# A layer norm's square root taken from the activation table, and the second block's norm moved ahead of the feed-forward steps, in an attention and feed-forward kernel

## The chip, the core and the metric

The kernel runs on one core of a Trainium2 chip. The metric is the device time of one execution in microseconds (us). The engines are named as the profile names them: PE (TensorE's matmuls) and PEld (its weight loads), DVE (VectorE), ACT (ScalarE), POOL (GpSimd), and SP (SyncE), whose queue issues nearly all of the transfers. Each engine works through its own instructions strictly in the order in which the program gives them; an instruction that waits for another engine holds up everything behind it on its own engine.

## The reference

The input x has 8 sequences of 256 tokens with 512 features, 2048 tokens in all. What is computed, shortened:

```python
xn = _layernorm(x, axis=-1)                  # (x - m) / sqrt(v + 1e-5)
s = attn(xn)                                 # latent attention, 128 heads, head size 4, rope part 64
g = _silu(ffn(xn))                           # gate = silu(lin1(xn)); up = lin3(xn); lin2(gate * up)
return x + s * g

def lin(x, wq, A, B):                        # each of lin1, lin2, lin3
    w = jnp.tile(wq, (1, 4))
    return x @ w.T + (x @ A.T @ B.T) * 0.5
```

Because the weight is tiled four times, a product with it is a product of the sum of the four quarters of x with `wq`. The kernel uses this: it sums the quarters first.

## The kernel before

**First phase and attention.** The kernel has two parts. `first_phase` handles the norm, the low-rank parts and the whole feed-forward network (FFN); it writes the gates g and the projected latents to DRAM. The attention over 64 pairs of (sequence, group of heads) follows and takes most of the time. The change touches the first phase alone, which covers about the first 200 us of the span, and within it what happens up to about 45 us.

**Blocks and tiles.** `first_phase` works on four blocks `tb` = 0 to 3 of 512 tokens. A block of x is four tiles `xt_tb_n` of 128 tokens by 512 features (`load_x`). The tag `xt` has six buffers, so four tiles of block 0 and two of block 1 have room at once; the third and the fourth tile of block 1 wait until tiles of block 0 have been transposed.

**The norm.** `norm_part(tb, n)` takes mean and variance of one tile on DVE (L416, L417). `norm(tb)` does this for four tiles and then finds 1/sqrt(variance + eps) for 128 x 4 values at once. It starts from the guess by a shifted integer (L428, L430) and improves it by three Newton steps: for block 0 as nine small DVE instructions (L436 to L438), for the other blocks as twelve small POOL instructions (L440 to L443), with two more (L449, L450) for the offset `off` = -mean/deviation. `norm_one(tb, n)` then normalizes a tile in place, on DVE for block 0 (L459), on ACT for the others (L457, which reads `off`). `turn(tb)` transposes the four tiles on PE, and ACT and DVE copy the results out of PSUM (L470, L472).

**Sums and narrow products.** `sums(tb)` adds the four quarters of the features: `xs0` on DVE (L479), `xs2` on POOL (L480), and their sum on DVE (L481). `narrow(tb)` makes the low-rank parts (`pm` on PE, `mid` on DVE L497), sends two rows through DRAM to spread them over all partitions (`low`), and `down(tb)` makes the latents (`pp`) and, on POOL, four differences for the attention (L158).

**Removing the first row.** Before block 0's FFN the weights `w1_sb` and `w3_sb` are changed once: the first row of `wq` is spread over the partitions by small PE products (`spread_first`, L627), copied by ACT into `first_0` and `first_1` (L635, L651), and subtracted by `less_first` (L641, L643: POOL for `w1_sb`, DVE for `w3_sb`) and `rest_less_first` (L652, L655, POOL). `first_0` and `first_1` lie in the two buffers of the tag `hT`, which the FFN needs afterwards.

**The FFN.** `main(tb, u)` is one of six steps of a block, each with two chunks of 128 hidden units (the last with one). Per chunk PE makes `px` and `py` in two PSUM banks, DVE adds the low-rank part to each (L541 for `gate`, L545), ACT applies SiLU to `gate` (L544), and the product of the two is made by POOL (L558) or DVE (L556). In steps 0 and 1 of block 0 both products are DVE's, and `py` is kept in PSUM until then. The tag `gate` has two buffers, PSUM has eight banks. `fold` (POOL) and `low_out` (PE, L582) follow after steps 3 and 5; `gate_out` makes the block's output (`pf`).

**The order.** Nothing is scheduled automatically (`tc.manual_schedule()`): the order of the Python calls is the order on each engine. Around the change the calls run thus: 26 transposes of a constant on PE (`warm(26)`); four `spread_first` with their copies; `warm(2)`; `norm(0)`; four `norm_one(0, n)`; `turn(0)`; `sums(0)`; `less_first(0)` on POOL; `narrow(0)`; `less_first(1)` on DVE; `down(0)`; `rest_less_first`; and then the loop over blocks and steps. In this loop, block 1's norm stands behind step 1 of block 0:

```python
if u == 1 and tb == 0:
    stats = norm(1)
if more:
    for n in range(4):
        if u == (n if tb else 2 + n // 2):
            norm_one(tb + 1, n, *stats)
```

SP's queue issues, in this order: block 0's four tiles, small weights, `wdn_sb`, ten loads of `w1_sb` and `w3_sb`, six small loads of `chunk_rows`, block 1's four tiles, and then `narrow(0)`'s transfers.

Of the kernel before, what the change touches and what calls it, by code (L numbers as in the profile page):

```python
# [9 lines left out]
F32 = mybir.dt.float32  # L10
I32 = mybir.dt.int32
AF = mybir.ActivationFunctionType
ALU = mybir.AluOpType
# [3 lines left out]
P = 128  # L17
# [20 lines left out]
def mla_ffn_gate_kernel(  # L38
# [19 lines left out]
    nc = tc.nc  # L58
# [255 lines left out]
    def first_phase(between):  # L314
# [13 lines left out]
        f2 = pool("f2", 2, st)  # L328
        xts, xns, xnT, xsum, lows = {}, {}, {}, {}, {}

        def load_x(tb):
            xts[tb] = []
            for n in range(4):
                t = f1.tile([P, D], F32, tag="xt", name=f"xt_{tb}_{n}", bufs=6)
                nc.sync.dma_start(out=t, in_=x[ds(tb * TB + n * P, P), :])
                xts[tb].append(t)

        def by_chunks(to, of):

# [18 lines left out]
        nc.scalar.dma_start(out=rows[64:97:32], in_=b13[0:33:32, :])  # L358
        for k, wt in enumerate((w1t, w3t)):
            nc.scalar.dma_start(out=rows[65 + 32 * k : 66 + 32 * k], in_=wt[0:1, :])  # L360
        chunk_rows = f2.tile([P, TB], F32, tag="gs", name="chunk_rows")[:, 0:P]
        nc.gpsimd.memset(chunk_rows[0:32], 0.0)

# [26 lines left out]
        nc.sync.dma_start(out=wdn_sb, in_=w_down.rearrange("(c p) m -> p c m", p=P))  # L390
        for w_sb, wt in ((w1_sb, w1t), (w3_sb, w3t)):
            load_chunks(nc.sync, w_sb, wt)

        of = b13[1:34:32, :].rearrange("k (q f) -> q k f", q=4)
        for n in range(2):
# [5 lines left out]
        for m in range(3):  # L401
# [2 lines left out]
                out=chunk_rows[16 + 2 * m : 18 + 2 * m, 96 : 96 + w],  # L404
                in_=of[3, :, ds(256 + 32 * m, w)],
            )
        load_x(1)

        mvs = {}

        def norm_part(tb, n):

            if n == 0:
                mvs[tb] = f2.tile([P, 4, 2], F32, tag="mv", name=f"mv_{tb}")
            s6 = f2.tile([P, 6], F32, tag="st", name=f"st_{tb}_{n}")
            nc.vector.bn_stats(s6, xts[tb][n])  # L416
            nc.vector.bn_aggr(mvs[tb][:, n, :], s6)  # L417

        def norm(tb):


            for n in range(4):
                norm_part(tb, n)
            mv = mvs[tb]
            ve = f2.tile([P, 4], F32, tag="ve", name=f"ve_{tb}")
            nc.vector.tensor_scalar_add(ve, mv[:, :, 1], EPS)
            i0 = f2.tile([P, 4], I32, tag="i0", name=f"i0_{tb}")
            nc.vector.tensor_single_scalar(i0, ve.bitcast(I32), 1, ALU.logical_shift_right)  # L428
            r0 = f2.tile([P, 4], I32, tag="r0", name=f"r0_{tb}")
            nc.vector.tensor_scalar(r0, i0, -1.0, float(0x5F3759DF), ALU.mult, ALU.add)  # L430
            r = r0.bitcast(F32)
            e = f2.tile([P, 4], F32, tag="e", name=f"e_{tb}")
            for step in range(3):
                new = f2.tile([P, 4], F32, tag=f"r{step}", name=f"r_{tb}_{step}")
                if tb == 0:
                    nc.vector.scalar_tensor_tensor(e, r, -0.5, r, ALU.mult, ALU.mult)  # L436
                    nc.vector.scalar_tensor_tensor(e, e, 1.0, ve, ALU.mult, ALU.mult)
                    nc.vector.scalar_tensor_tensor(new, e, 1.5, r, ALU.add, ALU.mult)  # L438
                else:
                    nc.gpsimd.tensor_mul(e, r, r)  # L440
                    nc.gpsimd.tensor_mul(e, e, ve)
                    nc.gpsimd.tensor_scalar(e, e, -0.5, 1.5, ALU.mult, ALU.add)
                    nc.gpsimd.tensor_mul(new, e, r)  # L443
                r = new

            off = None
            if tb:
                off = f2.tile([P, 4], F32, tag="off", name=f"off_{tb}")
                nc.gpsimd.tensor_mul(off, mv[:, :, 0], r)  # L449
                nc.gpsimd.tensor_scalar(off, off, -1.0, None, ALU.mult)  # L450
            return mv, r, off
# [22 lines left out]
        def sums(tb):  # L474

            a = xnT[tb]
            xs = [f1.tile([P, TB], F32, tag=f"xs{k}", name=f"xs{k}_{tb}") for k in range(2)]
            xs2 = f1.tile([P, TB], F32, tag="tmp", name=f"xs2_{tb}")
            nc.vector.tensor_add(xs[0], a[:, 0, :], a[:, 1, :])  # L479
            nc.gpsimd.tensor_add(xs2, a[:, 2, :], a[:, 3, :])  # L480
            nc.vector.tensor_add(xs[0], xs[0], xs2)  # L481
            nc.scalar.copy(xs[1], xs[0])
            xsum[tb] = xs
# [142 lines left out]
        def spread_first(k, ps, one, two):  # L626
            nc.tensor.matmul(  # L627
                ps, others[64 + 32 * k : 66 + 32 * k], two, start=True, stop=True, skip_group_check=True
            )
            return one, ps  # L630

        for i in range(2):
            for k in range(2):
                ps = bank(f"first_{k}_{i}").rearrange("p (q m) -> p q m", q=2)
                nc.scalar.copy(*spread_first(k, ps, *parts[k][i]))  # L635
        warm(2)

        def less_first(k, engine):
            w_sb = (w1_sb, w3_sb)[k]
# [14 lines left out]
                one = w_sb[:, 8:11][:, a, b]  # L654
                nc.gpsimd.tensor_sub(one, one, firsts[k][:, 8:11][:, a, b])  # L655

        stats = norm(0)
        for n in range(4):
            norm_one(0, n, *stats)
        turn(0)  # L660
        sums(0)
        less_first(0, nc.gpsimd)
        narrow(0)
        less_first(1, nc.vector)
        between(-1)
        for to, of in ((a2_sb, a2), (w2_sb, w2t), (w2_sb[96:98, 2, :], b2[0:2, :])):
            nc.sync.dma_start(out=to, in_=of)
# [3 lines left out]
        nc.scalar.copy(bcol_sb.rearrange("p c k -> p (c k)"), ps)  # L671
        rest_less_first(0)
        rest_less_first(1)
        for tb in range(NTB):
            more = tb + 1 < NTB
            for u in range(6):
                pj = None
                if not more and u >= 2:
                    pj = Project(u - 2)
                    pj.start()  # L680
                main(tb, u)
                if pj:
                    pj.second()
                    pj.end()
                if u in (3, 5):
                    fold(tb, u // 2 - 1)
                    low_out(tb, u // 2 - 1)
                if u == 1 and tb == 0:
                    stats = norm(1)
                if more:  # L690
                    for n in range(4):
                        if u == (n if tb else 2 + n // 2):
                            norm_one(tb + 1, n, *stats)
                if u == 4 and more:
# [429 lines left out]
```

## Time and profile before

| What | us |
|---|---|
| Median of 3 runs | 1986.38 (1986.12 to 1987.19) |
| The profiled execution's own time | 1985.42 |
| Span of that execution, first to last instruction | 1983.6 |
| PE busy in the span | 1966.4 |
| From 11 to 37 us: PE busy | 25.89 of 26.00 |
| From 37 to 50 us: PE busy | 8.60 of 13.00 |
| From 50 to 66 us: PE busy | 16.00 of 16.00 |
| From 200 to 1970 us: PE busy | 1768.37 of 1770.00 |

The rows for stretches come from the windows of the profile. They say where TensorE has gaps at all: at the very start, between 37 and 50 us, a little in each later block of the first phase, and hardly ever in the attention. ACT loads an activation table three times (L635 at 4.02 us, L544 at 23.77 us, and L717 ahead of the attention), 1.28 us each. PE's granted clock is full in all but a few microseconds of the span (mean 0.999).

### The profile page before, as it was taken

The numbers are of one execution on the slowest core, as the hardware profiler recorded it, in microseconds if no ns is written. First come the engines' busy times: TensorE is split into PE (matmuls) and PEld (weight loads), VectorE is DVE, ScalarE is ACT, GpSimd is POOL, SyncE is SP. The second block draws the span as 40 slices with busy tenths as digits, with TensorE's granted clock in tenths as the row PEclk, the third lists the DMA queues.
The fourth block names the chain that finished last, engine by engine and source line by source line (L and its number), as shares of the span: only waits on it lengthen the run. The fifth ranks groups of instructions, "written<-read, shape, count | busy, mean of one in ns | idle before, by whom it ended". The sixth has DMA issues, their size and how long they took to land.

```text
span 1983.6 us, 86719 instructions
## 1 busy us (share of the span) xinstructions
PE 1966.4 (99%) x38065; PEld 1402.2 (71%) x38065; DVE 1570.7 (79%) x2666; ACT 1091.5 (55%) x2987; POOL 759.1 (38%) x1113
## 2 busy tenths in 40 slices
PE   8999999999999999999999999999999999999998
PEld 4334577777777767777777767777777767777775
DVE  6764678888787877788787877788787878888888
ACT  3333556556556555556556555556556555655654
POOL 5876545554552323232332323232332323232232
PEclk9999999999999999999999999999999999999999
DMA  6235322212232223221232223221232222222212
GB/s 195 100 118 181 112 88 87 88 67 87 88 126 77 100 87 109 93 87 66 87 113 80 100 87 107 94 88 66 88 110 82 99 88 87 67 88 87 74 49 87
DMA packets 120048, 187.53 MB, mean 95 GB/s; under 512 B 10715, under 2 KB 84843, under 8 KB 119673
## 3 DMA queue, kind: packets, MB, share of 16 engines
q1 hardware_dynamic: 119665, 181.97, 26.7%
q8 instruction: 301, 4.93, 1.0%
q14 instruction: 74, 0.61, 0.1%
q10 hardware_dynamic: 8, 0.02, 0.0%
HBM read 147.86 MB, written 34.10 MB: 92 GB/s over the span
## 4 chain that ended last, share of the span: by engine, by line
PE 92%; POOL 3%; DVE 2%; issue 1%; DMA 1%; ACT 0%; SPq 0%; POOLq 0%; ACTq 0%; DVEq 0%
PE q L173 40%; PE sc L824 35%; PE av L870 11%; PE po L173 2%; PE pf L173 1%; PE py L173 1%; PE px L173 1%; PE qq L249 1%; POOL h4b L571 0%; DVE pt L853 0%; POOL h L570 0%; POOL hT L558 0%; DMA xt<-in_x_dram 0%; DMA gate_d<-gs 0%; POOL h L572 0%
## 5 line engine op out<-in xcount | busy, mean ns | idle before, releaser
L843 ACT ACTIVATE pr<-sc,nmx 128x256 f32<-128x256 f32 x2048 | 814.4, 500 | 470.3 <-DVE nmx L837 466.0
L837 DVE TENSOR_REDUCE nmx<-sc 128x2 f32<-128x512 f32 x1024 | 635.7, 683 | 289.1 <-PE sc L824 265.0
L853 DVE STREAM_TRANSPOSE pt<-pr 128x512 f32<-128x512 f32 x1024 | 635.1, 678 | 0.0
L216 POOL TENSOR_TENSOR e<-e,e 128x256 f32<-128x256 f32 x128 | 93.9, 733 | 1045.2 <-ACT e L211 559.3
L824 PE MATMUL sc<-act,qr 32*128 32x256 f32 x8192 | 489.0, 374 | 0.0
L173 PE MATMUL q<-x,ws 128*32 128x256 f32 x8192 | 488.9, 379 | 0.0
L824 PEld LDWEIGHTS sc<-act,qr 32*128 32x128 f32 x8192 | 421.2, 185 | 21.9
L173 PEld LDWEIGHTS q<-x,ws 128*32 128x32 f32 x8192 | 266.3, 110 | 175.7
L173 PE MATMUL q<-x,w 128*32 128x256 f32 x6144 | 381.6, 381 | 0.7 <-DVE py L545 0.7
L173 PEld LDWEIGHTS q<-x,w 128*32 128x32 f32 x6144 | 187.1, 110 | 155.7 <-ACT pr L843 35.9
L824 PE MATMUL sc<-kc,qcm 32*128 32x256 f32 x4096 | 281.3, 387 | 0.2 <-issue 0.2
L870 PE MATMUL av<-pt,vpad 128*32 128x128 f32 x8192 | 235.9, 273 | 0.1
L870 PEld LDWEIGHTS av<-pt,vpad 128*32 128x32 f32 x8192 | 226.3, 110 | 12.6 <-issue 1.6
L824 PEld LDWEIGHTS sc<-kc,qcm 32*128 32x128 f32 x4096 | 198.2, 184 | 52.2 <-issue 39.4
L211 ACT COPY e<-q 128x256 f32<-128x256 f32 x512 | 202.2, 396 | 25.9 <-PE q L173 25.8
L890 ACT ACTIVATE acc<-av,sides_sb 128x256 f32<-128x256 f32 (+1 forms) x130 | 54.2, 469 | 247.0 <-PE av L870 247.0
L269 POOL TENSOR_TENSOR qcm<-qc,mask_sb 128x1024 f32<-128x1024 f32 x64 | 122.2, 1910 | 0.0
L218 POOL TENSOR_TENSOR qr<-e,e 128x256 f32<-128x256 f32 x128 | 93.6, 731 | 10.0
L217 POOL TENSOR_TENSOR e<-e,e 128x256 f32<-128x256 f32 x128 | 93.6, 731 | 10.0
L310 POOL COPY vpad<-vall 32x128 f32<-32x128 f32 x256 | 74.9, 293 | 10.7 <-PE av L870 2.7
L228 DVE TENSOR_TENSOR qr<-e,q 128x256 f32<-128x256 f32 x128 | 53.9, 421 | 22.4 <-POOL e L216 17.0
L541 DVE SCALAR_TENSOR_TENSOR gate<-low,bcol_sb,px 128x512 f32<-128x512 f32 x44 | 32.8, 745 | 45.0 <-POOL hT L558 24.7
(124 smaller groups left out, 1133.7 us busy)
## 6 DMA issues: line engine op xcount, KB each, us to landing
w<-in_w_rope_dram SPq DMA_DIRECT2D x128, 512.0 KB
ws<-sums_d SPq DMA_DIRECT2D x96, 512.0 KB
sums_d<-ws SPq DMA_DIRECT2D x32, 512.0 KB
x<-xs_d SPq DMA_DIRECT2D x28, 256.0 KB
xt<-in_x_dram SPq DMA_DIRECT2D x16, 256.0 KB
xs_d<-xt SPq DMA_DIRECT2D x16, 256.0 KB
gate_d<-gs SPq DMA_DIRECT2D x16, 256.0 KB
g<-gate_d SPq DMA_DIRECT2D x16, 256.0 KB
```

Source lines behind the costliest of these rows:

```text
L173: nc.tensor.matmul(to[tile_], w[:, tile_], x, start=start, stop=stop, skip_group_check=True)
L211: nc.scalar.copy(self.e[i], self.banks[i])
L216: nc.gpsimd.tensor_add(m6, m6, m1)
L217: nc.gpsimd.tensor_add(m7, m7, m6)
L218: nc.gpsimd.tensor_add(self.out(1, 1), self.split(m7), self.split(m5))
L269: nc.gpsimd.tensor_mul(qcm, qks[b, sg // 2][0].rearrange("p (q i) -> p q i", i=32).unsqueeze(2).to_broadcast([P, 8, 4, 32]), mask_sb[:, ds ...
L310: nc.gpsimd.tensor_copy(vpad[rows, :, :, 8 * t + 4 * (sg % 2) :][..., :4], valls[b][rows, :, sg])
L824: nc.tensor.matmul(sc[r][:, h, :], lhs.rearrange("p t i -> p (t i)"), rhs, start=(part == 0 and h == 0), stop=(part == 2), skip_group_chec ...
L837: nc.vector.tensor_reduce(nmx[:, r, :], scs[n, f][r], AX.X, ALU.max, negate=True)
L843: nc.scalar.activation(p[:, h, :], scs[n, f][r][:, h, :], AF.Exp, bias=nmxs[n, f][:, r, h : h + 1])
L853: nc.vector.transpose(pts[n, f // 2, r].rearrange("p k q i -> p q k i")[:, ds(2 * (f % 2), 2)], prs.pop((n, f, r)).rearrange("p h (k j) -> ...
L870: nc.tensor.matmul(av[32 * r : 32 * r + 32, ds(half * P, P)], vpad[:, k, r, :], pt[r][:, k].rearrange("p q i -> p (q i)"), start=(k == 0), ...
```

## The change

It has five parts. The table's square root of a constant is taken once at the start (`one`), and for block 0 the guess and three Newton steps are replaced by a square root on ACT, a reciprocal on DVE and one Newton step on DVE. `norm(0)` is called after the first of the four copies of `first`, and the two warming transposes `warm(2)` go. Block 1's tiles 0 and 1 are loaded ahead of the `chunk_rows` loads, 2 and 3 in their old place. Block 1's four `norm_part` are put between `sums(0)`, `narrow(0)` and `less_first` (0 within `sums`, 1 ahead of `less_first(0)`, 2 and 3 behind `less_first(1)`). The rest of `norm(1)`, with its steps on POOL, comes ahead of the loop over steps, and `norm_one(1, n)` follows step n as in the other blocks, where it came after steps 2 and 3.

```diff
-        def load_x(tb):
-            xts[tb] = []
-            for n in range(4):
+        def load_x(tb, tiles=range(4)):
+            for n in tiles:
...
-                xts[tb].append(t)
+                xts.setdefault(tb, []).append(t)
...
+        one = f2.tile([P, 1], F32, tag="sq", name="one")
+        nc.gpsimd.memset(one, 1.0)
+        nc.scalar.activation(one, one, AF.Sqrt)
...
             load_chunks(nc.sync, w_sb, wt)
+        load_x(1, range(2))
...
-        load_x(1)
+        load_x(1, range(2, 4))
...
-            for n in range(4):
-                norm_part(tb, n)
+            if tb != 1:
+                for n in range(4):
+                    norm_part(tb, n)
...
-            i0 = f2.tile([P, 4], I32, tag="i0", name=f"i0_{tb}")
...
-            r = r0.bitcast(F32)
             e = f2.tile([P, 4], F32, tag="e", name=f"e_{tb}")
-            for step in range(3):
+            if tb:
+                i0 = f2.tile([P, 4], I32, tag="i0", name=f"i0_{tb}")
...
+                r = r0.bitcast(F32)
+            else:
+                sq = f2.tile([P, 4], F32, tag="i0", name="sq")
+                nc.scalar.activation(sq, ve, AF.Sqrt)
+                r = f2.tile([P, 4], F32, tag="r0", name="r_first")
+                nc.vector.reciprocal(r, sq)
+            for step in range(3 if tb else 1):
...
             nc.vector.tensor_add(xs[0], a[:, 0, :], a[:, 1, :])
+            if tb == 0:
+                norm_part(1, 0)
             nc.gpsimd.tensor_add(xs2, a[:, 2, :], a[:, 3, :])
...
+        copies = []
         for i in range(2):
             for k in range(2):
                 ps = bank(f"first_{k}_{i}").rearrange("p (q m) -> p q m", q=2)
-                nc.scalar.copy(*spread_first(k, ps, *parts[k][i]))
-        warm(2)
+                copies.append(spread_first(k, ps, *parts[k][i]))
+        nc.scalar.copy(*copies[0])
+        stats = norm(0)
+        for copy in copies[1:]:
+            nc.scalar.copy(*copy)
...
-        stats = norm(0)
         for n in range(4):
             norm_one(0, n, *stats)
         turn(0)
         sums(0)
+        norm_part(1, 1)
         less_first(0, nc.gpsimd)
         narrow(0)
         less_first(1, nc.vector)
+        norm_part(1, 2)
+        norm_part(1, 3)
...
         rest_less_first(1)
+        stats = norm(1)
         for tb in range(NTB):
...
-                if u == 1 and tb == 0:
-                    stats = norm(1)
                 if more:
                     for n in range(4):
-                        if u == (n if tb else 2 + n // 2):
+                        if u == n:
                             norm_one(tb + 1, n, *stats)
```

More of the change, by code (lines that the diff above doesn't have):

```diff
@@ L426, in norm @@
             nc.vector.tensor_scalar_add(ve, mv[:, :, 1], EPS)
-            i0 = f2.tile([P, 4], I32, tag="i0", name=f"i0_{tb}")
-            nc.vector.tensor_single_scalar(i0, ve.bitcast(I32), 1, ALU.logical_shift_right)
-            r0 = f2.tile([P, 4], I32, tag="r0", name=f"r0_{tb}")
-            nc.vector.tensor_scalar(r0, i0, -1.0, float(0x5F3759DF), ALU.mult, ALU.add)
-            r = r0.bitcast(F32)
-            e = f2.tile([P, 4], F32, tag="e", name=f"e_{tb}")
-            for step in range(3):
+            e = f2.tile([P, 4], F32, tag="e", name=f"e_{tb}")
+            if tb:
+                i0 = f2.tile([P, 4], I32, tag="i0", name=f"i0_{tb}")
+                nc.vector.tensor_single_scalar(i0, ve.bitcast(I32), 1, ALU.logical_shift_right)
+                r0 = f2.tile([P, 4], I32, tag="r0", name=f"r0_{tb}")
+                nc.vector.tensor_scalar(r0, i0, -1.0, float(0x5F3759DF), ALU.mult, ALU.add)
+                r = r0.bitcast(F32)
[5 more added lines that the diff above has]
+            for step in range(3 if tb else 1):
                 new = f2.tile([P, 4], F32, tag=f"r{step}", name=f"r_{tb}_{step}")
```

## The prediction

> **What bounds the kernel now.** I read the page first. TensorE is busy almost without a break, so a microsecond is won only where TensorE waits, or where something that it will wait for is made earlier.
>
> ```profile
> PE 1966.4 (99%) x38065; PEld 1402.2 (71%) x38065; DVE 1570.7 (79%) x2666; ACT 1091.5 (55%) x2987; POOL 759.1 (38%) x1113
> ```
>
> Next I read the timeline of TensorE over the first 125 us, which is where every edit lies, and looked for the starts with idle time before them (start, length, engine, line, names; the bracket is the idle time and its releaser).
>
> ```profile
> 9.38 0.44 PE L615 MATMUL idle<-ident 128*128 128x128 f32 x2
> 11.12 3.45 PE L467 MATMUL xpt<-ident,xt 128*128 128x128 f32 x16 [1.30 <-DVE xt L459]
> ...
> 38.20 1.06 PE L582 MATMUL pm<-hT,a_sb 128*32 128x512 f32 x8 [1.18 <-DVE gate L541]
> ...
> 43.52 1.07 PE L173 MATMUL py<-xs,w_sb 128*32 128x512 f32 x8 [1.68 <-DVE gate L541]
> ...
> 46.38 1.28 PE L467 MATMUL xpt<-ident,xt 128*128 128x128 f32 x8 [0.78 <-DVE hT L556]
> 48.27 1.06 PE L173 MATMUL px<-xs,w_sb 128*32 128x512 f32 x8 [0.60 <-DVE gate L541]
> ```
>
> From 11.12 to 36.97 TensorE never waits. Between 37 and 49 it waits four times, always for VectorE. The bracket leaves out the overlap of neighbours; by start-to-start times (a group of eight FFN matmuls every 0.86 us, a tile of four transposes about 0.52) what is lost from 36.83 to 50.34 is 1.37 + 1.87 + 0.13 + 0.83 + 0.85 + 0.33 = 5.4 us. VectorE's and GpSimd's timelines say why.
>
> ```profile
> 33.59 0.69 DVE L416 BATCH_NORM_STATS2 st<-xt 128x6 f32<-128x512 f32 x1
> ...
> 37.40 0.74 DVE L541 SCALAR_TENSOR_TENSOR gate<-low,bcol_sb,px 128x512 f32<-128x512 f32 x1
> ...
> 42.71 0.75 DVE L541 SCALAR_TENSOR_TENSOR gate<-low,bcol_sb,px 128x512 f32<-128x512 f32 x1 [2.60 <-POOL hT L558]
> ```
>
> ```profile
> 28.96 1.22 POOL L655 TENSOR_TENSOR w_sb<-w_sb,first 128x264 f32<-128x264 f32 x3
> 37.57 0.20 POOL L440 TENSOR_TENSOR e<-r 128x4 f32<-128x4 f32 x1 [7.39 <-DVE r L430]
> ...
> 41.22 0.23 POOL L450 TENSOR_SCALAR off<-off 128x4 f32<-128x4 f32 x1
> 41.41 2.50 POOL L558 TENSOR_TENSOR hT<-gate,hT 128x512 f32<-128x512 f32 x2
> ```
>
> The second block's statistics and first Newton guess hold VectorE from 33.59 to 37.40 (3.8 us) between FFN steps 1 and 2; GpSimd's 14 small steps, 37.57 to 41.45 (3.88 us), then stand ahead of step 2's product L558, which alone frees the `gate` buffer for step 3 (42.71). GpSimd was idle for 7.39 us before them.
>
> **The change, part by part.**
>
> (1) First norm. Before, L426 starts at 8.08 and norm_one (L459) at 10.51. Nine Newton steps every 0.196 us and two guess steps go; one square root, one reciprocal and three Newton steps stay. The square root stands on ScalarE behind the first of the four `first` copies (L635, start 8.37, next start some 0.51 later), so it starts at 8.9. No row has it; a ScalarE instruction on 32 columns takes 0.19 us (L671), one on one column 0.20 (L717): 0.2, so 9.1. The reciprocal of 4 columns has no row either: between 0.16 (any VectorE step on 4) and 0.95 (L908 on 128 columns); it is near the first, and I take 0.2 with 0.05 for the change of engine: 9.35. Three steps: 9.94. The norm starts 0.57 us earlier (0 to 0.7). The other three copies come 0.2 later, at most 10.7; their first reader is GpSimd after 17.
>
> (2) The early square root of `one`. Its table load is the one that ScalarE already makes: L635's ACT_TABLE_LOAD, 1.28 us at 4.02, in a stretch where ScalarE has nothing until 8.37. If that cover went it would cost 1.28. I take zero, provided that one table serves copy and square root; otherwise see rival C.
>
> [...] The trace shows 1.28 us loads and cannot yet show a square root's.
>
> (3) TensorE's clock. Windows view (length, busy of PE, PEld, DVE, ACT, POOL, granted clock, DMA share, GB/s):
>
> ```profile
> 10.50:10.80 0.30, 0.00 (x0) 0.00 (x0) 0.29 (x1) 0.00 (x0) 0.00 (x0) 0.97 0.87 238
> 10.80:11.00 0.20, 0.00 (x0) 0.00 (x0) 0.20 (x2) 0.00 (x0) 0.00 (x0) 0.50 0.93 312
> ...
> 14.00:14.20 0.20, 0.20 (x3) 0.20 (x2) 0.00 (x0) 0.20 (x1) 0.00 (x0) 0.51 0.01 2
> 14.20:14.40 0.20, 0.20 (x3) 0.12 (x1) 0.00 (x0) 0.20 (x1) 0.00 (x0) 1.00 0.09 9
> ```
>
> The clock is halved from about 10.8 to 14.2, which covers the first transposes: 0.21 us each, against 0.13 later. The two warming transposes (9.38) go, so the idle time before is 9.4 to 10.55 instead of 9.8 to 11.12, about as long; I let the clock fall at the same moment. Transposes from 10.55 then run 0.3 us at full speed and end near 13.76, 0.75 earlier; the `pm` matmuls behind them run half-fast until 14.2, so TensorE keeps about 0.48 of it. GpSimd and VectorE, which follow the transposes, get 0.75.
>
> [...]
>
> (4) norm_part(1,0..3): eight instructions, 4 x (0.69 + 0.1) = 3.2 us of VectorE, moved from 33.6 into its idle times: 0 behind the first sum (it waits 1.17 us for L480 there; the tile must have landed by 15.4, and is now issued at 10.9 instead of 14.54), 1 ahead of `mid` (L497 would be ready at about 17.7 and goes at 18.05, still no later than now), 2 and 3 into the 2.36 us that VectorE waits at 24.28. The first FFN gate slips to 25.0 at most; its products wait for a `hT` buffer held by GpSimd until 28 anyway. Without that cover it would cost 0.7.
>
> (5) DMA. SP issues two x tiles ahead of the chunk_rows loads (0.9 us later, end 15.4; needed at 21), the other two at 15.4 to 16.3 as now. SP then waits for `mid` anyway. Zero.
>
> (6) GpSimd's chain: L480 starts 0.75 earlier. But VectorE's subtractions (L643) now meet it at other moments. Side by side, such steps took GpSimd 1.71 to 1.79 us instead of 1.28; the new positions give back between 0 and 0.35: I take 0.2. L655 ends 0.55 earlier than 30.18, at 29.63, and the 14 Newton steps run straight behind: `off` at 33.53.
>
> (7) The new wait. norm_one(1,0) is now in ScalarE's queue behind step 0, ahead of step 1's two SiLUs (30.60 and 31.92 now). It must wait for `off`: 33.56; the SiLU follows 0.72 later (two such norms took 1.52), ends 34.91. Queued behind it: VectorE's two products L556 (34.97 instead of 32.40), which free the two `py` banks; TensorE, which reaches step 3's `py` at 33.77, waits for 35.7, **1.93 us of new waiting**.
>
> (8) From there: two L556, 1.19 to the next start: 36.16 for step 2's gate (37.40 before). Gate to SiLU 0.83, SiLU 0.63, to L558 0.15: 37.77 (41.41 before, GpSimd now being free). L558 to step 3's gate 1.30: **39.07, against 42.71: 3.64 us earlier**. What follows on VectorE, ScalarE and GpSimd (products, folds, second sums) is a chain without slack in the rows and keeps the 3.64. TensorE allows it: 0.48 + 5.38 - 1.93 = 3.9, less 0.3 that stays at step 5. The matmuls of `pf`, GpSimd's queue (no idle time from 41.41 to 76.4) and what follows shift together.
>
> Sum: -3.64 on the span of 1983.6, that is 1979.96. That execution took 1985.42, so 1981.8; the median of the runs shown is 0.96 above that execution: **1982.7**. A measurement of this kernel can tell 0.2%, 4.0 us, from no change, and the forecast lies just inside that.
>
> **The rivals.**
>
> [...]
>
> C: the square root brings a table load of its own into the norm's path, because copies and square root do not share a table, or the early one is not kept. One load of 1.28 us (L635) takes back more than part (1): -3.64 + 1.28 = -2.4, 1984.0. For: the trace has three loads, for copy, SiLU and exponential, and nothing on square roots. Against: the same ScalarE runs copies between SiLUs without a load.
>
> D, the other side: statistics wait for their tiles. VectorE runs in order, so a late xt_1_3 holds the FFN's first gate. It decides only from a point: the steps from the first gate to step 1's products take 7.2 us and are needed by 34.97, so the gate may start at 27.7 and the tile may land at about 25.4 at no cost; a landing at 29 eats the gain, one at 34 gives +5, 1991. For: two of the tiles wait on SP for the first block's transposes. Against: today the same four are issued from 14.54 to 16.3, and the DMA share is down to 0.31 by 19 to 20 us.
>
> **How the numbers follow.** The forecast's mechanism 0.60, B 0.20, C 0.13, D 0.07. The forecast's own range: 0.57 of part (1) may be 0 (then -3.0); no GpSimd collision and a quicker square root give -4.6; 3.97 lies inside, and because the uncollided values are cheap to reach I put 0.32 of the 0.60 beyond it and 0.28 within. Faster by over 0.2%: 0.32 + 0.20 = 0.52. Within: 0.28 + 0.13 = 0.41. Slower: 0.07. The range runs from all of TensorE's gaps closed (0.48 + 5.38 = 5.9, 1980.5) to C with the largest collision and no gain left of part (1) (-1.6, 1984.8).
>
> **What would show it.** L459 near 9.9; transposes ending near 13.8; statistics of block 1 between 15 and 25 on VectorE; GpSimd's Newton steps at about 29.7 to 33.5; ScalarE's first L457 near 33.6, with step 1's SiLU behind it; TensorE waiting some 1.9 us at `py` near 34 to 36, and nothing of the waits at 38.2 and 43.5; step 3's gate at 39. The prediction is wrong if a table load stands between L635's copies, if the Newton steps start after 33, or if TensorE's shift at the first `pf` matmul (58.95) is not that of the whole span.

## The result and the profile after

| | median, us | lowest to highest | executions |
|---|---|---|---|
| Before | 1985.88 | 1984.37 to 1987.42 | 22 |
| After | 1984.07 | 1980.74 to 1985.20 | 22 |

The ratio of after to before is 0.9988, with a 95% interval of 0.9983 to 0.9994: 2.4 us less, between 1.2 and 3.4. That lies within the 0.2% (4.0 us) named in the prediction, so it counts as no change that one such measurement can tell, though the interval leaves zero out. Measured again later beside a before of 1986.07, the kernel took 1983.75, a ratio of 0.9990 [0.9981, 0.9999].

The profiled execution of after took 1984.70 us, its span is 1982.8. That is only 0.8 below the span of before, less than the medians differ by: of 22 executions this one lies 0.6 above the median. So single spans are read here only for *where* time went; how much comes from the ratios.

The busy time of TensorE is the first row to compare, from the page of after.

```profile
PE 1968.0 (99%) x38063; PEld 1415.6 (71%) x38063; DVE 1572.0 (79%) x2659; ACT 1092.3 (55%) x2989; POOL 760.2 (38%) x1114
```

VectorE has seven instructions fewer, ScalarE two more (the two square roots), TensorE two fewer (the warming transposes). TensorE is no less busy than before; its gaps had to shrink for the kernel to gain. The timeline of TensorE in after shows which did (start, length, engine, line, names, count; the bracket is the idle time before it and what ended it).

```profile
6.41 1.12 PE L640 MATMUL first<-rows,others 2*128 2x512 f32 x2
8.23 2.93 PE L640 MATMUL first<-rows,others 2*128 2x512 f32 x6 [0.70 <-DMA rows<-in_w3t_dram]
11.09 3.67 PE L478 MATMUL xpt<-ident,xt 128*128 128x128 f32 x16
...
36.27 1.06 PE L173 MATMUL px<-xs,w_sb 128*32 128x512 f32 x8 [0.22 <-DVE hT L569]
```

```profile
45.15 1.06 PE L173 MATMUL px<-xs,w_sb 128*32 128x512 f32 x8 [0.60 <-DVE gate L554]
...
74.75 1.07 PE L173 MATMUL py<-xs,w_sb 128*32 128x512 f32 x8 [1.78 <-ACT gs L621]
```

The transposes of block 0 (L478) start at 11.09, where they started at 11.12 before, although their input is ready much earlier: the products of `first` (L640) stand ahead of them in the queue, and six of those wait 0.70 us for a small load. From 37 to 50 us the gaps are nearly gone, as the windows say (length, busy of PE, PEld, DVE, ACT, POOL, granted clock, DMA share, GB/s); 12.27 of 13.00 us stand against 8.60 before.

```profile
11.00:37.00 26.00, 25.78 (x246) 11.45 (x249) 20.57 (x34) 10.52 (x21) 17.01 (x31) 0.91 0.54 172
37.00:50.00 13.00, 12.27 (x128) 5.09 (x128) 12.56 (x19) 7.75 (x13) 11.28 (x9) 1.00 0.59 200
```

ScalarE, VectorE and GpSimd around the moved steps, from the timelines of after:

```profile
4.31 1.28 ACT L363 ACT_TABLE_LOAD   x1 [4.31 <-DMA rows<-in_b_dram]
...
8.29 0.21 ACT L441 ACTIVATE sq<-ve 128x4 f32<-128x4 f32 x1
...
24.53 1.28 ACT L557 ACT_TABLE_LOAD   x1
...
34.16 0.81 ACT L468 ACTIVATE xt<-xt,off,r 128x512 f32<-128x512 f32 x1 [4.29 <-POOL off L461]
34.88 1.13 ACT L557 ACTIVATE gate<-gate 128x512 f32<-128x512 f32 x2
```

```profile
25.01 0.75 DVE L431 TENSOR_SCALAR ve<-mv 128x4 f32<-128x4 f32 x1
25.79 1.20 DVE L435 TENSOR_SCALAR i<-ve 128x4 int32<-128x4 int32 x1
27.02 0.35 DVE L437 TENSOR_SCALAR r<-i 128x4 int32<-128x4 int32 x1
27.15 0.75 DVE L554 SCALAR_TENSOR_TENSOR gate<-low,bcol_sb,px 128x512 f32<-128x512 f32 x1
...
35.53 1.28 DVE L569 TENSOR_TENSOR hT<-gate,py 128x512 f32<-128x512 f32 x2 [1.82 <-ACT gate L557]
...
39.60 0.75 DVE L554 SCALAR_TENSOR_TENSOR gate<-low,bcol_sb,px 128x512 f32<-128x512 f32 x1 [0.16 <-POOL hT L571]
```

```profile
25.69 1.27 POOL L158 TENSOR_TENSOR xt<-act,xt 128x512 f32<-128x512 f32 x1
...
30.25 0.20 POOL L451 TENSOR_TENSOR e<-r 128x4 f32<-128x4 f32 x1
...
33.90 0.23 POOL L461 TENSOR_SCALAR off<-off 128x4 f32<-128x4 f32 x1
38.28 2.60 POOL L571 TENSOR_TENSOR hT<-gate,hT 128x512 f32<-128x512 f32 x2 [4.15 <-ACT gate L557]
```

The chain of the prediction is there link by link: Newton steps on GpSimd from 30.25 instead of 37.57, ScalarE's norm of block 1 held until `off` comes (34.16) with step 1's SiLUs right behind it (34.88), the products L569 behind those (35.53), and step 3's gate at 39.60 instead of 42.71: 3.11 us earlier.

By the end of the span only 0.8 of those 3.11 are left. The way to see where they went is to take the same instruction at several points of the program and subtract its start in before from its start in each kernel. The next table does that for all profiles, in us; each is one execution.

| Kernel | first norm | transposes start | step 3's gate | block 2's first `px` | first exponential | 65th exponential | span |
|---|---|---|---|---|---|---|---|
| before (start) | 10.51 | 11.12 | 42.71 | 112.93 | 221.59 | 271.02 | 1983.63 |
| after | -1.15 | -0.02 | -3.11 | -2.08 | -2.30 | -1.24 | -0.80 |
| after, again | -1.06 | -1.06 | -4.16 | -3.52 | -3.33 | -2.55 | -2.01 |
| e1 | -1.25 | -1.25 | -4.70 | -3.27 | -3.44 | -3.43 | -3.90 |
| e2 | -0.59 | -0.27 | -3.38 | -3.40 | -2.72 | -2.52 | -3.22 |
| e3 | -1.41 | -0.85 | -0.76 | +0.14 | -0.16 | +1.07 | +0.15 |
| e4 | -0.32 | -0.32 | -0.17 | -0.11 | -1.06 | -1.06 | -0.16 |
| e5 | -1.44 | +0.18 | -4.84 | -3.26 | -3.83 | -3.83 | -3.18 |
| e7 | -1.63 | -1.57 | -6.95 | -5.87 | -6.82 | -6.83 | -7.25 |
| e8 | -0.11 | -0.12 | -5.10 | -4.79 | -4.54 | -4.20 | -4.89 |
| e9 | -0.89 | -0.87 | -4.08 | -4.07 | -5.08 | -4.50 | -5.25 |
| e10 | -1.41 | -1.34 | -7.04 | -6.51 | -8.26 | -7.73 | -7.08 |
| e11 | -0.17 | -0.15 | -6.44 | -6.52 | -8.79 | -6.99 | -4.60 |
| e12 | -1.20 | +0.83 | +1.02 | +1.32 | +1.03 | +1.13 | +0.54 |

Two places take most of it back in both executions of after: between step 3 and block 2 (1.03 and 0.64 us), and between the 33rd and the 65th exponential at the entry of the attention (1.05 and 0.79). Behind the 65th exponential another 0.44 and 0.54 go, which no experiment here followed up.

The first is a transfer. SP's queue in block 1 sends two rows of `mid` to DRAM (`low_d`) and reads them back spread out (`low`). In before the second issue follows the first by 1.67 us, in after by 2.42. First SP's queue in before, then in after:

```profile
62.01 0.53 SPq L499 DMA_DIRECT2D low_d<-mid  x1
63.68 0.80 SPq L503 DMA_DIRECT2D low<-low_d  x2
```

```profile
59.11 0.53 SPq L512 DMA_DIRECT2D low_d<-mid  x1
...
61.53 0.80 SPq L516 DMA_DIRECT2D low<-low_d  x2
```

The second lies in SP's queue too: 32 issues of `wo_sb` stand ahead of the issue of `w`, which the projections of q need. First SP's queue in before, then in after:

```profile
227.28 12.28 SPq L804 DMA_DIRECT2D wo_sb<-in_w_o_dram  x32
239.78 0.57 SPq L124 DMA_DIRECT2D w<-in_w_rope_dram  x1
```

```profile
225.46 12.89 SPq L822 DMA_DIRECT2D wo_sb<-in_w_o_dram  x32
238.44 0.57 SPq L124 DMA_DIRECT2D w<-in_w_rope_dram  x1
```

TensorE comes to that stretch 2.29 us earlier, `w` is issued only 1.34 earlier, and a wait that before does not have appears:

```profile
245.72 2.80 PE L173 MATMUL q<-x,ws 128*32 128x256 f32 x48 [0.67 <-POOL ws L137]
```

### The profile page after: what moved, and what is told of

Its sections match the earlier page's. It is cut to its first block, busy times and chain, and to the rows that moved or that the text cites. A ratio compares the mean times of both kernels' runs of the same rounds, so it can differ in the third digit from the quotient of the medians.

```text
span 1982.8 us, 86707 instructions
## 1 busy us (share of the span) xinstructions
PE 1968.0 (99%) x38063; PEld 1415.6 (71%) x38063; DVE 1572.0 (79%) x2659; ACT 1092.3 (55%) x2989; POOL 760.2 (38%) x1114
## 4 chain that ended last, share of the span: by engine, by line
PE 92%; POOL 3%; DVE 2%; issue 1%; DMA 1%; SPq 0%; ACT 0%; POOLq 0%; ACTq 0%; DVEq 0%
PE q L173 40%; PE sc L842 35%; PE av L888 11%; PE po L173 2%; PE pf L173 1%; PE qq L249 1%; POOL h4b L584 0%; PE px L173 0%; DVE pt L871 0%; POOL h L583 0%; PE py L173 0%; POOL hT L571 0%; POOL h L585 0%; PE vps L294 0%; POOL xt L158 0%
## 5 line engine op out<-in xcount | busy, mean ns | idle before, releaser
L173 PEld LDWEIGHTS q<-x,ws 128*32 128x32 f32 x8192 | 271.6, 110 | 171.8 <-POOL ws L137 1.1
L173 PEld LDWEIGHTS q<-x,w 128*32 128x32 f32 x6144 | 191.5, 110 | 151.1 <-ACT pr L861 34.6
```

The costliest lines, as they stand in the source:

```text
L173: nc.tensor.matmul(to[tile_], w[:, tile_], x, start=start, stop=stop, skip_group_check=True)
```

## The experiments

Twelve runs follow, of eleven other kernels and of after once more, in three groups, each on one chip beside the kernel before. Times are medians; "us less" is the ratio turned into time on the median of before in that group (1985.33 for e1 to e4, 1985.06 for e5 to e9, 1986.07 for e10 to e12 and after). Two letters occur in what was expected: theory K is that the two warming transposes, which the change drops, kept TensorE's clock, and that the clock lost takes the gain of the earlier start; theory L is that the longer way of `low_d` in block 1 comes from a load of instruction code that falls between its two rows.

**The two halves of the change alone.** e2 is before with the tiles of block 1 loaded in two parts, its `norm_part` calls moved, `norm(1)` ahead of the FFN and `norm_one(1, n)` at step n; the first norm is the old one.

```diff
+            if tb == 0:
+                norm_part(1, 0)
...
+        norm_part(1, 1)
...
+        norm_part(1, 2)
+        norm_part(1, 3)
...
+        stats = norm(1)
         for tb in range(NTB):
...
-                        if u == (n if tb else 2 + n // 2):
+                        if u == n:
```

> Only the move of block 1's norm (tiles loaded earlier, statistics among the first sums, Newton steps ahead of the FFN, norm_one behind its own step); the first norm and the two warming transposes as before. By the forecast's sum this is 3.64 less the 0.55 that GpSimd's chain got from the start: -3.1. If the start of the changed kernel loses what it should win (theory K), this half does better than the whole change: -2.6 to -3.4. If the loss is in the transfers later (rival T), it does no better than the change: -1.2 to -2.4.

e3 is before with the first norm by the table's square root, called behind the first copy, and with `warm(2)` kept.

```diff
+        nc.scalar.copy(*copies[0])
+        stats = norm(0)
+        for copy in copies[1:]:
+            nc.scalar.copy(*copy)
         warm(2)
```

> Only the first norm by the table's square root, called behind the first of the copies; warming transposes kept, block 1's norm where it was. Forecast's terms (1) and (3): -0.5 to -0.75, all of it at the start. Rival: the transposes stand on TensorE behind the four products of `first`, which wait for three small loads; the norm comes 1.15 us earlier (9.36 instead of 10.51 in the profile after) but the transposes do not (11.09 instead of 11.12): 0, within 0.3.

e2 took 1981.75, a ratio of 0.9983 [0.9974, 0.9991]: 3.4 us less. e3 took 1985.03, 0.9999 [0.9990, 1.0008]: nothing. The move of block 1's norm brings the whole gain, and the early start none at the end. The 3.4 us of e2 are what theory K expected of it; e1 and e4 below test that theory directly. Yet in the trace of e3 it did start the work earlier. The two rows are TensorE's in e3:

```profile
6.41 3.45 PE L636 MATMUL first<-rows,others 2*128 2x512 f32 x8
...
10.27 3.62 PE L476 MATMUL xpt<-ident,xt 128*128 128x128 f32 x16
```

The transposes start 0.85 earlier here, and step 3's gate is still 0.76 earlier. Block 1 then takes 0.9 back (its `low_d` takes 2.35 us to the second issue, as in after, not 1.67), and the entry of the attention another 1.23.

**The warming transposes.** e1 is after with them put back, e4 is before without them.

```diff
                 copies.append(spread_first(k, ps, *parts[k][i]))
+        warm(2)
         nc.scalar.copy(*copies[0])
```

> The changed kernel with the two warming transposes put back behind the four products of `first`. Measured for the change itself: ratio 0.9988, about -2.4 us, where -3.6 was forecast. Theory K (clock): the missing 1.2 us is TensorE's halved clock at the start, which the change makes longer (one stretch of 3.4 us in the profile before, two in the profile after), because less work keeps the engine busy there. Two more transposes of 0.2 us then shorten it in part of the executions: -2.8 to -3.6 against the kernel before. Rival T (transfers): the start is not at fault, the rest is lost in blocks 1 to 3 and in the attention on transfers that land at other moments; then this kernel is within 0.5 us of the change, -1.9 to -2.9, and mean granted clock is as in the change.

```diff
-        warm(2)
```

> The kernel before without the two warming transposes, nothing else. Theory K: TensorE has less to do between 9.4 and 11.1, the clock falls in more executions or for longer: +0.5 to +2.0, with a mean granted clock below that of before. Rival T: two transposes more or less in a stretch of idling change nothing: within 0.3 us, same clock.

e1 took 1983.00, 0.9987 [0.9978, 0.9996], 2.6 us less than before, as after itself; e4 1985.74, 1.0003 [0.9994, 1.0012]. Neither shows theory K. In the profiles the clock was halved at the start for 3.4 us in before (10.8 to 14.2) and for 6.8 in after (9.05 to 15.88), but also for 6.8 in e2, e3 and e12, which have the two transposes, and in e4, which hasn't; in e1 for 3.4. So the two transposes don't decide it. Nor does the clock hold the missing gain: in the last group the executions with a mean clock of 0.998 took 1984.10 us on average in after and 1986.15 in before, those with 0.999 took 1983.60 and 1985.41, about 2 us less either way. The halved stretch in after, by its windows:

```profile
8.50:9.00 0.50, 0.50 (x4) 0.21 (x2) 0.41 (x3) 0.00 (x0) 0.38 (x4) 1.00 1.10 326
9.00:9.50 0.50, 0.50 (x3) 0.24 (x1) 0.43 (x3) 0.01 (x1) 0.38 (x4) 0.55 1.10 204
15.00:15.50 0.50, 0.50 (x8) 0.20 (x4) 0.49 (x1) 0.00 (x0) 0.00 (x0) 0.50 0.02 4
15.50:16.00 0.50, 0.50 (x12) 0.26 (x8) 0.40 (x1) 0.00 (x0) 0.35 (x1) 0.62 0.01 1
```

The last column but two is the one to read: 1.00 falls to 0.55 while TensorE is fully busy with products that use two rows of its array, and the clock is back only within 15.5 to 16. When it falls for one stretch of 3.4 us and when for two is taken up at the end.

**The new wait on ScalarE.** e5 is after with the old places of `norm_one(1, n)`, behind steps 2 and 3; e8 is e2 with the same.

```diff
-                        if u == n:
+                        if u == (n if tb else 2 + n // 2):
```

> The changed kernel with block 1's norm_one back behind steps 2 and 3 (two each), so that ScalarE does not wait for `off` ahead of step 1's SiLUs. Forecast's term (7) says that this wait delays VectorE's products L569 by 2.5 us and with them steps 2 and 3: in the changed kernel's profile VectorE idles 1.82 us there (35.53) and step 3's first gate is at 39.60. Without it the products follow their gates at about 33.7, step 3's gate comes at about 37.8, and TensorE, then next to bind, keeps about 1.0 of the 1.8: 1.0 us less than the change, about -3.4 against the kernel before. Rival: TensorE had no wait worth the name there (0.22 us at 36.27), so that the order of norm_one is worth nothing: -2.4 as the change.

> The kernel of e2_ffn_only (first norm as before, block 1's norm moved; measured ratio 0.9983, about -3.4) with norm_one behind steps 2 and 3 as before. By term (7) again 1.0 us less: -4.4. Rival: as e2_ffn_only, -3.4.

e5: step 3's gate at 37.88, 1.72 earlier than in after; 1982.21, 0.9983 [0.9974, 0.9992], 3.4 us less than before, as expected. e8: the gate at 37.62, 1.71 earlier than in e2; 1979.92, 0.9971 [0.9960, 0.9983], 5.8 us less, more than the 4.4 expected. The norms then stand where nothing waits for them. The timeline of ScalarE in e5:

```profile
33.33 0.63 ACT L557 ACTIVATE gate<-gate 128x512 f32<-128x512 f32 x1 [0.69 <-DVE gate L554]
...
37.16 0.63 ACT L557 ACTIVATE gate<-gate 128x512 f32<-128x512 f32 x1 [0.69 <-DVE gate L554]
37.70 1.50 ACT L468 ACTIVATE xt<-xt,off,r 128x512 f32<-128x512 f32 x2
```

Step 1's second SiLU runs at 33.33, where in after the first waits until 34.88, and TensorE has no gap from 29.8 to 43.8. So the wait that part (7) named costs after 1.7 us at step 3; at the end the gain is 1.0 from after to e5 and 2.4 from e2 to e8, with intervals that overlap.

e5 and e8 also answer what the early start is worth, since they ran in one group and differ in nothing else: e5 has the table's square root and the early `norm(0)`, e8 the old first norm with `warm(2)`. The early start makes the kernel 2.3 us slower there (1982.21 against 1979.92; ten of e5's eleven executions took longer than the slowest of e8's six, 1980.53). Their profiles put most of it in block 1: between step 3 and block 2 e5 gives back 1.58 us and e8 0.31, and `low_d` takes 2.66 us in e5 and 1.67 in e8.

**What stands ahead of the transposes.** e7 is e5 with the products of `first` and their copies called behind `turn(0)`, and 40 instead of 26 transposes of the constant at the start.

```diff
-        warm(26)
+        warm(40)
...
         turn(0)
+        copies = []
+        for i in range(2):
+            for k in range(2):
...
+                copies.append(spread_first(k, ps, *parts[k][i]))
+        for copy in copies:
+            nc.scalar.copy(*copy)
```

> The kernel of e5_late_norm, and the four products of `first` with their copies behind the first block's transposes instead of ahead of them, with 40 warming transposes instead of 26 so that TensorE is kept busy until the norm is done. If the earlier norm (9.36 instead of 10.51) was worth nothing because the transposes stood behind these products on TensorE and behind their loads, the transposes now start at about 9.9, at full clock, and end near 12.3 instead of 14.8; the products' 2.3 us come behind them. Expected -4.5 to -6 against the kernel before. If the products only change places with the wait: -3.4, as e5_late_norm.

It took 1979.13, 0.9970 [0.9958, 0.9981]: 6.0 us less. TensorE's timeline in e7, and the windows of its idle stretch:

```profile
9.54 2.08 PE L478 MATMUL xpt<-ident,xt 128*128 128x128 f32 x16 [1.76 <-DVE xt L470]
11.55 1.99 PE L640 MATMUL first<-rows,others 2*128 2x512 f32 x8
13.47 3.66 PE L173 MATMUL pm<-act,ck_sb 128*32 128x256 f32 x64
```

```profile
7.50:9.50 2.00, 0.28 (x3) 0.04 (x1) 1.55 (x8) 0.20 (x1) 1.54 (x9) 1.00 1.11 305
```

The transposes start 1.57 earlier than in before and run at 0.13 us each, with the granted clock at 1.00 throughout (16 took 3.67 us in after, at 0.50); they end at 11.62, 2.94 earlier. The eight products take 1.99 us, where six took 2.93 in after. All six executions of e7 had a mean clock of 1.000; nearly all of before and after have 0.998 or 0.999. The edit thus does two things at once, and how the 3.1 us between e5 and e7 (1982.21 and 1979.13) divide between the order of the work and the kept clock is not separated: the two of e5's executions that kept a mean clock of 1.000 took 1979.37 and 1980.54, its two shortest, where e7's took 1977.91 to 1981.10.

**Is it the start, then?** e11 is e8 with the products of `first` moved in the same way (64 transposes of the constant at the start), that is, e7 with the old first norm.

```diff
-        warm(26)
+        warm(64)
...
-        for i in range(2):
-            for k in range(2):
-                ps = bank(f"first_{k}_{i}").rearrange("p (q m) -> p q m", q=2)
-                nc.scalar.copy(*spread_first(k, ps, *parts[k][i]))
-        warm(2)
...
         turn(0)
+        for i in range(2):
+            for k in range(2):
+                ps = bank(f"first_{k}_{i}").rearrange("p (q m) -> p q m", q=2)
+                nc.scalar.copy(*spread_first(k, ps, *parts[k][i]))
```

> The kernel of e8_move_late (ratio 0.9971; first norm by nine Newton steps as before) with the four products of `first` behind the transposes and 64 warming transposes. It tells what the table's square root is worth once the transposes don't stand behind these products: the norm starts at about 10.4 here and at 8.9 in e10_later_six, and everything behind follows it. Expected 1.3 to 1.6 us above e10_later_six, about -5.3 against the kernel before. Rival: the earlier norm is not worth anything even then (GpSimd's chain is held by something else): same as e10_later_six.

It took 1980.87, 0.9975 [0.9966, 0.9984]: 5.0 us less, against 6.2 for e10 in the same group (below). The transposes end 1.12 later than in e10, and the medians differ by 1.9. The direction is that of a square root which pays once nothing stands ahead of the transposes; the intervals overlap, so its size is not settled. Against its own base e8 (0.9971 [0.9960, 0.9983], 5.8 us less in its group) e11 gains nothing that can be told: step 3's gate comes 1.34 earlier than in e8, but in e11's profile 4.2 of the 8.8 us by which its first exponential is early are gone at the end. So moving the products of `first` paid beside the new first norm (e5 to e7) and is not seen to pay beside the old one.

**The code load.** Each of e9, e10 and e12 adds six more square roots of `one` at the very start, where ScalarE has time; they stand ahead of every later instruction of ScalarE, and the rest of the program is the same. e9 is e1 with them, e10 is e7, e12 is e3.

```diff
         nc.scalar.activation(one, one, AF.Sqrt)
+        for _ in range(6):
+            nc.scalar.activation(one, one, AF.Sqrt)
```

> The kernel of e1_warm_back (the change with the warming transposes) with six more square roots of the constant on ScalarE, at about 5.8 to 7 us, where it waits. They compute nothing that is used. In the profiles of the three kernels with the table's square root, block 1's `low_d` goes to memory and back in 2.35 to 2.66 us, with a load of 8 KB of code between its two rows; in the three without, in 1.67, with that load behind it. Theory L: two instructions more on ScalarE move this code load onto the transfer, and block 1 loses about 0.8 us by it. Six more move it away again: round trip 1.67, TensorE's wait for gs in block 1 about 1.0 to 1.2 instead of 1.95, and -3.2 instead of the -2.6 of e1_warm_back. Rival: the round trip has nothing to do with ScalarE's instructions, it stays at 2.3 or more, and the time that of e1_warm_back.

> The kernel of e7_first_later (ratio 0.9970, block 1's `low_d` 2.41 us there and back) with the six square roots more of e9_six_more on ScalarE. If both findings hold together, the round trip is 1.67 again, block 1 gives back 0.7 us less: -6.5 to -7 against the kernel before, where e7_first_later had -6.0. Rival: block 1 is bound by GpSimd and the copies of the gate there, and not by this transfer: -6.0, as e7_first_later.

> The kernel of e3_norm_only (first norm by the table's root alone; ratio 0.9999) with six square roots more on ScalarE. If the code load on block 1's transfer took back what the norm won, the norm alone is now worth what the forecast said, -0.5 to -0.75. If the products of `first` in front of the transposes are the reason, it is still 0 within 0.3.

First SP's queue in e1 and what the DMA engines moved from 57.4 to 60.2 us there (40 slices, GB/s, and the queue that carries instruction code):

```profile
57.47 0.53 SPq L512 DMA_DIRECT2D low_d<-mid  x1
...
60.13 0.80 SPq L516 DMA_DIRECT2D low<-low_d  x2
```

```profile
GB/s 0 0 0 0 0 0 0 0 0 0 0 0 0 0 0 0 0 29 117 0 0 0 0 0 0 0 0 29 0 0 0 0 0 0 0 0 0 0 0 0
...
q14 instruction: 1, 0.01, 1.4%
```

Then the same in e9, from 58 to 59.9 us:

```profile
58.12 0.53 SPq L514 DMA_DIRECT2D low_d<-mid  x1
...
59.79 0.80 SPq L518 DMA_DIRECT2D low<-low_d  x2
```

```profile
GB/s 0 0 0 0 0 0 0 172 0 0 0 0 0 0 0 0 0 0 0 0 0 0 0 0 0 0 0 43 43 0 0 0 0 0 0 0 0 0 0 0
...
q14 instruction: 1, 0.01, 1.4%
```

In e1 the load of 8 KB of code (the larger number) comes right behind the first row of `low_d`, and the second row lands ten slices, 0.7 us, behind it. In e9 the code comes before both rows, which land together. The way takes 2.66 us in e1, 1.67 in e9; 2.41 in e7, 1.66 in e10; 2.35 in e3, 1.67 in e12. Every kernel with exactly the two square roots of the change has the long way, and every one without them, or with six more, has the short one. So theory L agrees with all the traces, and from e1 to e9 the place of the code load itself is seen to change with the number of ScalarE's instructions, some 50 us behind them. What the six more do is isolated by the pairs; that the first two brought the load there is read from kernels that differ in VectorE's steps as well.

TensorE's wait for `gs` in block 1 and the time that block 1 gives back go with it. First e1, then e9:

```profile
73.27 1.14 PE L173 MATMUL py<-xs,w_sb 128*32 128x512 f32 x8 [1.95 <-ACT gs L621]
```

```profile
72.81 1.06 PE L173 MATMUL py<-xs,w_sb 128*32 128x512 f32 x8 [0.64 <-ACT gs L623]
```

Between step 3 and block 2, e1 gives back 1.43 us and e9 0.01; e7 gives back 1.08 and e10 0.53; e3 gives back 0.90 and e12 0.30. Behind this wait e1's clock was halved once more, from 74.1 to 77.5 us: two groups of eight FFN matmuls took 1.95 and 1.88 us there, where the next took 1.04.

What it costs in the medians is less clear. e9 took 1981.12, 0.9982 [0.9973, 0.9990], 1.0 us better against before than e1. But e10, 1979.01 and 0.9969 [0.9956, 0.9981], is no better than e7 (0.9970), and e12, 1986.04 and 1.0001 [0.9992, 1.0010], is as e3. In e12's profile it is the products of `first` that took the start away: six of them waited 0.88 us for the row of w3, and the transposes started at 11.94, later than in before.

**After, once more.** It ran in the third group as itself.

> The changed kernel itself, beside the three others. As measured: -2.4 (interval -3.4 to -1.2).

Its profile differs from the first one at the start: the products did not wait, the transposes began at 10.05, and step 3's gate was 4.16 earlier than in before. The span is 2.01 shorter, the ratio 0.9990.

## Why the prediction was near, and what failed in it

The forecast was 1982.7; 1984.07 was measured, in the range. The forecast of 3.64 us less stands against 2.4, and lies outside the interval of 1.2 to 3.4. The prediction had given 0.52 to a gain of more than 0.2% and 0.41 to one within it, which is what came.

**Part (1), right in kind, and larger.** The square root took 0.21 us at 8.29 (0.2 forecast), and the norm started at 9.36 and 9.45, not 9.94, because the first product came 0.7 to 0.8 us earlier in these executions as well, and with it the first copy (7.57 for 8.37 in after), so that the square root had only `ve` to wait for.

**Part (2), right.** One table serves copy and square root: there is a load at 4.31, ahead of the first square root (5.60), and none until SiLU's at 24.53, with copies from 7.57 on and the second square root (8.29) between. Rival C is out. Each of the two loads took 1.28 us, as in before, where SiLU's takes the time from 23.77 and the SiLU itself starts at 25.07.

**Part (3), wrong in its place.** It took the end of the first norm as what releases the transposes. The products of `first` stand ahead of them in TensorE's queue and ran until 11.16 in the first execution, so 1.15 us of earlier norm became 0.02 of earlier transposes and 0.53 of missing gain at step 3's gate (39.60 for 39.07). In the second execution no load was late, and the transposes kept 1.06. The clock did not fall at the same moment either; it fell during the products (at 9.05, in before at 10.79) and stayed down twice as long (6.83 us for 3.41). The 0.20 for B in the prediction's chances stood for a clock that stays full through the first transposes; no run isolates what keeps it there or moves its fall. What the runs showed is that with this change it is kept only now and then: three of after's 33 executions had a mean clock of 1.000 and took 1980.74, 1981.13 and 1981.91 us, while the others took 1981.56 to 1985.85. Of the 83 executions of before in the three groups none had it.

**Part (4), mis-sized, without consequence.** Block 1's statistics are hidden as said. But the three steps on 4 columns that follow took 0.75, 1.20 and 0.35 us, beside GpSimd's L158, and the first FFN gate was at 27.15 where I had 25.0 at most. The cover held: VectorE still waits 1.82 us ahead of L569. What lengthened the three steps no run isolates. In before, where GpSimd was idle beside them, they took 0.17 us each (36.91 to 37.49); in after the one of 1.20 us ended at 26.99, and the GpSimd step beside it, of 1.27 us, at 26.96.

**Parts (5) and (6).** No x tile was late, so rival D is out. The Newton steps began at 30.25 and 29.18, around the 29.63 of the forecast, the difference being that of the transposes.

**Part (7), right in order, wrong in TensorE's share.** Norm at 34.16 (33.56 forecast), the SiLU 0.72 behind, the products at 35.53 (34.97). TensorE's wait was forecast at 1.93 us and shows as 0.22 idle, since TensorE itself came to the FFN at 23.83, 0.76 later than in before where I had it 0.48 earlier (its clock was halved until 15.88, and its `pm` products took 4.22 us instead of 3.66), and needed the freed bank one group later. e5 and e8 show that the price of this wait was on the path all the same, 1.7 us by step 3's gate, through VectorE's products and not through TensorE.

**Part (8) is the step that failed.** At step 3's gate the two executions were 3.11 and 4.16 earlier, 3.64 on the mean, just the forecast. That is luck: one was 0.53 us late and the other 0.52 early, as their transposes had been (11.09 and 10.05 where 10.55 was forecast). "What follows shift together" is what does not hold: of these, 0.80 and 2.01 are left at the end. The prediction's own third sign says the same: TensorE's shift at the first `pf` matmul is 3.11 and 4.16, that of the whole span 0.80 and 2.01. Block 1 takes 0.64 to 1.03 back, by the pairs half of it or more through the longer way of `low_d`, which is gone in e9, e10 and e12; the entry of the attention takes 0.79 to 1.05, where `w` stands behind 32 issues. I had called the rest a chain without slack; a chain through a transfer on SP's queue is no such thing. The second loss is not settled: the 32 issues took between 11.99 (e5) and 13.42 us (e11), the loss was 0.01 at most in e1, e5 and e7, 1.23 in e3, 1.80 in e11, and whether anything in the change sets it was not tried.

**Versions that beat both.** e7 and e10, with the norms back behind steps 2 and 3 and the products of `first` behind the transposes, took 0.9970 [0.9958, 0.9981] and 0.9969 [0.9956, 0.9981] of before's time: about 6 us less, where the change as it was gave 2.4. e8 can't be told from them (0.9971 [0.9960, 0.9983]) and is far simpler: the first norm and the products stay as they were before, and only block 1's loads, statistics and Newton steps move.

## What to carry to other kernels

An earlier input is worth what the consumer's queue lets through: look at what stands ahead of it in order, there eight small products, before counting the gain. Test each half of a change alone and also inside the best version: the early start was worth nothing by itself (e3) and cost 2.3 us beside the late norms (e5 against e8). Moving a producer early is half of the edit; the reader must be placed where the result is already there (e5, e8), or the wait is moved into another queue. And take the shift between two profiles at several points of the program rather than at the end: it shows each place that gives time back, and needs no more than the same instruction's start in both.

## What the runs showed of the hardware

TensorE's clock fell from 1.00 to 0.55 within 9.0 to 9.5 us in after while TensorE was busy all through that stretch with two-row products, after 0.70 us of idling; in e3 it fell at the same moment with no wait in its timeline from 3.75 us on; and it stayed at 1.00 in e7 through 1.76 us of idling behind 40 full transposes. In the second execution of after it fell at 8.8, and TensorE had been busy from 4.60 on, so idle time just ahead of it did not bring it down there.

The time at half clock was 3.41 us in before (10.79 to 14.20) and e1 (9.28 to 12.69), and twice that, 6.83, in after (9.05 to 15.88); the windows of e2, e3, e4, e12 and the second execution of after give 6.8 as well. In the 3.41 us ahead of a fall, all matmuls but the two-row products of `first` took 0.44 us in before, 0.84 in after and 1.46 ahead of e1's second fall. In the first 3.41 us at half clock they took 3.08 us in before, where the full clock came next, and 1.38 in after and 2.68 in e3, where it did not. The transposes of block 0 began 0.3 us behind the fall in before and 0.6 in e1, and 1.2 (e3) to 3.3 us (e12) behind it in the six profiles with 6.8 us. What sets the fall and its length no run isolates.

The way of a 4 KB transfer in two rows (`low_d`) to memory and back took 2.35 to 2.66 us in six profiles and 1.66 or 1.67 in the eight others. In seven of them the DMA slices show where a load of 8 KB of instruction code fell: between the two rows in after, e1 and e3 (2.42, 2.66 and 2.35 us), behind them in before, e2 and e4 and ahead of them in e9 (1.67 us each). Six more instructions of 0.2 us on ScalarE were enough to move it away from there (e1 to e9).
